# A four-layer image kernel, layer 0: the depthwise convolution of half the keys moves from TensorE to nine taps on VectorE

## The chip, the cores and the metric

The kernel runs on one core of one Trainium2 chip. Its time is the device time of one execution in microseconds (us); lower is better. A "span" is the time from the first to the last instruction in one profiled execution.

## What is computed

The reference takes two images of 128 channels by 64 x 64 pixels and adds four layers to them, one after the other. Only layer 0 is touched here. Cut to what matters:

```python
xn  = biasfree_ln(group_norm(x), ln1_w)              # per pixel, over the 128 channels
qkv = einsum('oi,bihw->bohw', w_qkv, xn)             # 1x1: 128 -> 5*128 channels
qkv = conv(qkv, w_dw, 3x3, 'SAME', groups=5*128)     # depthwise: each channel by its own 9 taps
q1, k1, v, q2, k2 = split(qkv, 5)                    # groups 0..4 of 128 channels
q1, q2, k1, k2 = l2norm over the 4096 pixels, per channel
out = softmax(q1 k1^T * temperature) v + v softmax(q2^T k2 * temperature)
x   = x + conv1x1(biasfree_ln(conv1x1(out, w_po)), w_proj) + b_proj
```

All is float32. A depthwise convolution of one group and one half of an image (32 of the 64 rows) is called a piece here: 128 channels, 2048 output pixels, nine taps each.

## The kernel before

`_layer0` handles the two images in turn. For each it calls `convolutions` (the 1x1 and depthwise parts, called the convolution stage below), then `attention`, and last `finish` (output projections and the residual). `finish` of image 0 is not run at once: it is a generator, passed as `before` into the convolution stage of image 1 and stepped there.

**Pieces on TensorE.** Eight pieces, in the list `order`: `(1,0), (1,1), (0,0), (0,1), (3,0), (4,0), (3,1), (4,1)`, as (group, half); group 0 is q1, 1 is k1, 3 and 4 are q2 and k2. For each piece `pointwise` computes the 1x1 product into PSUM on TensorE (L1553) and ScalarE copies it into a frame in SBUF with a rim of zeros (L1560; POOL clears the rim, L1543 to L1546). A frame's product is called P below. Then `depthwise` computes the piece with 144 matmuls of 32 x 32 diagonal blocks (L1575), called D below, into two PSUM tiles: `ps[0]` and `ps[1]`. A diagonal block on another row strip of TensorE puts its rows at another place, so the results of q1 and k1 are put in order by `in_place`: eight ScalarE copies out of `ps[0]`, eight VectorE copies out of `ps[1]` (L1595), with four of each before and four after the next frame's first half. q2 and k2 stay permuted and are copied whole by `copy` (L1586), which alternates between ScalarE and VectorE. `squares` (L1600, ScalarE) sums the squares for the norms.

**Pieces on VectorE.** The two pieces of v (group 2) are computed by `value_taps` on VectorE, straight from two frames of the tag `vpad` into `v`: one multiplication (L1611) and eight multiply-and-adds in place (L1613), each over 128 x 2048 elements. `convolutions` steps this generator a fixed number of times at the end of each turn n of its loop, `(0, 0, 3, 3, 4, 4, 4, 0)[n]`.

**PSUM.** The pool `spp` has three buffers of two banks each, tag `sp`. Each P takes two of them in turn (and one column block of `acc0`), each D two at once; so a D can only start when two of the three are free, and a P needs one after the other.

**Order.** The context `_in_order` chains the instructions of each of TensorE, VectorE, ScalarE and POOL in the order in which the program issues them. What stands in one engine's queue behind a waiting instruction therefore waits as well. The order of `convolutions` is thus the order on each engine: in turn n the depthwise piece n, the frame of piece n+2, copies, squares; in turn 0 also both frames of v and six steps of `before`; in turn 1 the rest of `before`; in turn 3 the norms (`inverse_norm`, `sc`); in turn 4 the scaling of q1; in turns 5 to 7 the channel products (`products`) and the transposes of v (`value_tiles`); at the end of the turn the taps.

Of the kernel before, what the change touches and what calls it, by code (L numbers as in the profile page):

```python
# [12 lines left out]
ALU = mybir.AluOpType  # L13
# [3 lines left out]
B, C, H, W = 2, 128, 64, 64  # L17
S = H * W
CH = 512
# [1416 lines left out]
def _layer0(ctx, tc, X, a, cst, worst, there, dram):  # L1436
    nc = tc.nc
# [6 lines left out]
    def sp():  # L1444
        return spp.tile([128, 2, CH], F32, tag="sp", name="ps_sp")

    def acc(n):
        return accp.tile([128, CH], F32, tag=f"acc{n}", name=f"ps_acc{n}")
# [25 lines left out]
    k1 = one.tile([128, S], F32, name="k1")  # L1474
    v = one.tile([128, S], F32, name="v")
# [62 lines left out]
    def frame(pool, tag="pad", bufs=2):  # L1538
        return pool.tile([128, H // 2 + 2, W + 2], F32, tag=tag, name=tag, bufs=bufs)

    def pointwise(pad, grp, half):

        nc.gpsimd.memset(pad[:, :, 0:1], 0.0)  # L1543
        nc.gpsimd.memset(pad[:, :, W + 1 : W + 2], 0.0)
        edge = 0 if half == 0 else H // 2 + 1
        nc.gpsimd.memset(pad[:, edge, :], 0.0)  # L1546
        first, to = (0, 1) if half == 0 else (H // 2 - 1, 0)
        for r0 in range(0, H // 2 + 1, 2 * ROWS):
            n = min(2 * ROWS, H // 2 + 1 - r0)
            ps = sp() if n > 1 else acc(0).rearrange("p (o c) -> p o c", o=1)  # L1550
            for i in range(0, n, ROWS):
                rows = min(ROWS, n - i)
                nc.tensor.matmul(  # L1553
                    ps[:, i // ROWS, : rows * W],
                    w_qkv[:, grp * C : (grp + 1) * C],
                    xn[:, (first + r0 + i) * W : (first + r0 + i + rows) * W],
                    start=True,
                    stop=True,
                )
            nc.scalar.copy(  # L1560
                pad[:, to + r0 : to + r0 + n, 1 : W + 1],
                ps.rearrange("p k (h w) -> p (k h) w", w=W)[:, :n, :],
            )
            yield
# [32 lines left out]
    def squares(pool, t, at):  # L1597
        junk = pool.tile([128, 2 * CH], F32, tag="junk", name="junk", bufs=1)
        n = t.free_size()
        nc.scalar.activation(junk[:, :n], t, AF.Square, accum_out=at)  # L1600

    def value_taps(pads):

        for half in range(2):
            cols = slice(half * S // 2, (half + 1) * S // 2)
            out = v[:, cols].rearrange("p (h w) -> p h w", w=W)
            for t in range(9):
                x = pads[half][:, t // 3 : t // 3 + H // 2, t % 3 : t % 3 + W]
                tap = wd[:, 18 + t : 19 + t]
                if t == 0:  # L1610
                    nc.vector.tensor_scalar_mul(out, x, tap)  # L1611
                else:
                    nc.vector.scalar_tensor_tensor(out, x, tap, out, ALU.mult, ALU.add)  # L1613
                yield

    def value_tiles(half):
        for i in range(2):
            ps = sp()
            t0 = 16 * half + 8 * i
            for t in range(8):  # L1620
                nc.tensor.transpose(
                    ps[:, t // 4, t % 4 * 128 : (t % 4 + 1) * 128],
                    v[:, (t0 + t) * 128 : (t0 + t + 1) * 128],
                    ident,
                )
            copy(vt[:, t0 : t0 + 8, :], ps.rearrange("p k (t c) -> p (k t) c", c=C))
            yield

    def products(pool, qk, half, gram):

        tok = {}
        for r in range(5):
            if r < 4:
                ps = sp()
                for n in range(2):
                    for t in range(4):
                        nc.tensor.transpose(
                            ps[:, n, t * 128 : (t + 1) * 128],
                            qk[:, n, r, t * 128 : (t + 1) * 128],
                            ident,  # L1640
                        )
                tok[r] = pool.tile([128, 2, CH], F32, tag="tok", name="tok", bufs=2)
                copy(tok[r], ps)
            if r >= 1:
                x = tok.pop(r - 1)
                for t in range(4):
                    nc.tensor.matmul(
                        gram[:, (r - 1) * 128 : r * 128],
                        x[:, 1, t * 128 : (t + 1) * 128],
                        x[:, 0, t * 128 : (t + 1) * 128],  # L1650
                        start=(half == 0 and r == 1 and t == 0),
                        stop=(half == 1 and r == 4 and t == 3),
                    )
            yield

    def convolutions(pool, b, before):


        ss = small.tile([128, 2, 4], F32, tag="ss", name="ss")
        ss2 = small.tile([128, 2, 4, 2], F32, tag="ss2", name="ss2")  # L1660
        gram = acc(1)
        order = [(1, 0), (1, 1), (0, 0), (0, 1), (3, 0), (4, 0), (3, 1), (4, 1)]
        frames = [frame(pool) for _ in range(2)]
        for n in range(2):
            run(pointwise(frames[n], *order[n]))
        pads = [frame(pool, "vpad") for _ in range(2)]
        taps = value_taps(pads)
        qk = None
        for n, (grp, half) in enumerate(order):
            ps = depthwise(grp, frames.pop(0))  # L1670
            following = iter(())
            if n + 2 < len(order):
                frames.append(frame(pool))
                following = pointwise(frames[-1], *order[n + 2])
            if grp >= 3:
                if grp == 3:
                    qk = pool.tile([128, 2, 4, CH], F32, tag="qk2", name="qk2", bufs=1)
                for p in range(2):
                    copy(qk[:, grp - 3, 2 * p : 2 * p + 2, :], ps[p])
                run(following)  # L1680
                for r in range(4):
                    squares(pool, qk[:, grp - 3, r, :], ss2[:, grp - 3, r, half : half + 1])
            else:
                out = (q1, k1)[grp]
                in_place(ps, half, out, 0)
                next(following, None)
                in_place(ps, half, out, 1)
                run(following)
                for i in range(2):
                    at = 2 * half + i  # L1690
                    squares(
                        pool, out[:, at * 2 * CH : (at + 1) * 2 * CH], ss[:, grp, at : at + 1]
                    )
            if n == 0:
                for half in range(2):
                    run(pointwise(pads[half], 2, half))
                for _ in range(6):
                    next(before, None)
            elif n == 1:
                run(before)  # L1700
            if n == 5:
                run(products(pool, qk, 0, gram))
            elif n == 6:
                run(value_tiles(0))
            elif n == 7:
                run(value_tiles(1))
                run(products(pool, qk, 1, gram))
            if n == 3:
                nq = inverse_norm(ss[:, 0, :], "nq1")
                nk = inverse_norm(ss[:, 1, :], "nk1")  # L1710
                sc = small.tile([128, 1], F32, tag="sc", name="sc")
                nc.vector.scalar_tensor_tensor(sc, nq, nk, temp, ALU.mult, ALU.mult)
            if n == 4:
                for c in range(0, NCH, 2):
                    cols = slice(c * CH, (c + 2) * CH)
                    nc.vector.tensor_scalar_mul(q1[:, cols], q1[:, cols], sc)
            for _ in range((0, 0, 3, 3, 4, 4, 4, 0)[n]):
                next(taps, None)

        own = small.tile([128, 4, C], F32, tag="own", name="own", bufs=1)  # L1720
        nc.vector.tensor_mul(
            own,
            gram.rearrange("p (r c) -> p r c", r=4),
            blocks.unsqueeze(1).to_broadcast([128, 4, C]),
        )
        return ss2, own
# [152 lines left out]
    def run(gen):  # L1879
        for _ in gen:  # L1880
            pass

    def chain(*gens):
        for g in gens:
            yield from g
# [3 lines left out]
    with _in_order(tc):  # L1889
        first = normalize(0)  # L1890
# [11 lines left out]
        wd = one.tile([128, 45], F32, name="wd")  # L1902
# [559 lines left out]
```

## Time and profile before

| | us |
|---|---|
| three runs | 4122.99, 4132.37, 4132.41 |
| median of the three | 4132.37 |
| the profiled execution's own time | 4122.99 |
| its span | 4121.1 |
| convolution stage of image 0, first L1553 to first L1370 (the attention's first matmul) | 39.45 to 190.08 |
| convolution stage of image 1, with the `finish` of image 0 in it | 798.64 to 997.57 |

The profile is one execution seen by the hardware profiler. Its timeline lists, per engine, runs of like instructions: start, length in us, engine, line, operation, output and inputs with their shapes, how many, and in brackets how long the engine stood idle just before them and whose result ended that wait. One float32 matmul of the program is recorded as two matmul records, so a D of 144 matmuls shows as x288. "PEclk" is the TensorE clock granted, as a share of full speed.

### The profile page before, as it was taken

What the parts mean: (1) busy time and instruction counts of PE and PEld (TensorE: products, weight loads), DVE (VectorE), ACT (ScalarE), POOL (GpSimd) and SP (SyncE); (2) the same over time, 40 slices, a digit from 0 to 9 for tenths busy, and PEclk for the clock granted to TensorE, in tenths of its full rate; (3) what the DMA queues carried; (4) which work ended last, traced back from release to release, by engine and by line L of the source; (5) the groups of instructions that cost most, each with busy time, mean ns of one, the idle gap of its engine ahead of it and who ended that gap; (6) DMA issues with size and microseconds to landing.
All of it is one profiled execution on the core that took longest, in us unless ns stands there. A gap on an engine that the chain in (4) does not pass through costs nothing. (4 is left out here: it accounts for less than half of the span.)

```text
span 4121.1 us, 83188 instructions
## 1 busy us (share of the span) xinstructions
PE 3944.4 (96%) x35790; PEld 1382.1 (34%) x35790; DVE 3183.8 (77%) x3526; ACT 3228.6 (78%) x3907; POOL 72.2 (2%) x145
## 2 busy tenths in 40 slices
PE   7999999989999998997898999999999999999998
PEld 4522222245222223445665332223222332222222
DVE  4689999747989998986775878767777777766666
ACT  4478888734888884334654899999999999999998
POOL 1001000000000001000000000000000000000000
PEclk9999999999999999998998999999999999999999
DMA  1199970000000000003673211111112011110000
GB/s 49 24 192 180 181 104 2 2 2 2 2 2 2 1 2 13 0 1 132 254 281 104 74 32 34 43 43 32 32 34 67 19 32 32 36 53 6 6 6 4
DMA packets 193133, 217.66 MB, mean 53 GB/s; under 512 B 30441, under 2 KB 154345, under 8 KB 188658
## 3 DMA queue, kind: packets, MB, share of 16 engines
q1 hardware_dynamic: 192754, 212.25, 20.2%
q8 instruction: 282, 4.62, 0.5%
q14 instruction: 97, 0.79, 0.1%
HBM read 178.64 MB, written 98.57 MB: 67 GB/s over the span
## 5 line engine op out<-in xcount | busy, mean ns | idle before, releaser
L2181 ACT ACTIVATE weights<-ps_s 128x1024 f32<-128x1024 f32 x1920 | 1780.6, 1078 | 93.8 <-PE ps_s L2167 93.7
L1379 ACT ACTIVATE weights<-ps_s 128x1024 f32<-128x1024 f32 x1024 | 992.9, 1023 | 169.3 <-PE ps_s L1370 151.1
L2190 PE MATMUL ps_acc<-weights,vt 128*32 128x512 f32 x8192 | 1094.5, 606 | 0.0
L1827 DVE TENSOR_TENSOR sums<-sums,weights 128x2048 f32<-128x2048 f32 x384 | 880.0, 2292 | 43.7 <-ACT weights L1379 7.4
L2167 PE MATMUL ps_s<-q,k 64*128 64x512 f32 x4096 | 838.4, 472 | 6.3 <-DVE exp_i L2123 3.0
L2167 PEld LDWEIGHTS ps_s<-q,k 64*128 64x128 f32 x4096 | 352.7, 184 | 948.4 <-ACT weights L2181 824.7
L1370 PE MATMUL ps_s<-q,k 32*64 32x512 f32 x8192 | 631.5, 614 | 3.7 <-ACT weights L1379 1.5
L1787 PE MATMUL ps_acc<-weights,vt 128*32 128x512 f32 x4096 | 550.0, 605 | 7.2 <-ACT used L1817 3.7
L2139 DVE SCALAR_TENSOR_TENSOR exp_z<-exp_z,exp_m 128x1024 f32<-128x1024 f32 x384 | 469.7, 1223 | 11.2
L2123 DVE TENSOR_SCALAR exp_i<-ps_s 128x1024 int32<-128x1024 f32 x128 | 156.7, 1224 | 254.0 <-PE ps_s L2167 253.1
L1370 PEld LDWEIGHTS ps_s<-q,k 32*64 32x64 f32 x8192 | 162.0, 130 | 435.1 <-PE ps_s L1370 337.9
L2190 PEld LDWEIGHTS ps_acc<-weights,vt 128*32 128x32 f32 x8192 | 161.9, 108 | 304.2 <-issue 303.4
L1787 PEld LDWEIGHTS ps_acc<-weights,vt 128*32 128x32 f32 x4096 | 81.1, 108 | 426.6 <-issue 403.1
L662 DVE SCALAR_TENSOR_TENSOR X<-g,w,X 128x2048 f32<-128x2048 f32 x84 | 197.4, 2351 | 2.6
L1827 DVE TENSOR_TENSOR sums<-weights 128x2048 f32<-128x2048 f32 x64 | 146.6, 2291 | 62.8 <-ACT weights L1379 62.6
L2143 DVE SCALAR_TENSOR_TENSOR weights<-exp_z,exp_i 128x1024 f32<-128x1024 f32 x128 | 156.7, 1224 | 13.9
L1575 PE MATMUL ps_sp<-pad,diag 32*32 32x512 f32 x4608 | 159.8, 600 | 2.3 <-ACT q L1595 1.3
L2139 DVE SCALAR_TENSOR_TENSOR exp_z<-exp_m 128x1024 f32<-128x1024 f32 x128 | 155.9, 1218 | 0.0
L1008 PE MATMUL ps_z<-w_ri,e 128*32 128x128 f32 x2048 | 137.4, 409 | 14.5 <-DVE e L950 12.4
L1575 PEld LDWEIGHTS ps_sp<-pad,diag 32*32 32x32 f32 x4608 | 95.3, 103 | 55.5 <-issue 17.1
L950 DVE TENSOR_SCALAR e<-ps_pe 32x136 f32<-32x136 f32 (+1 forms) x352 | 104.4, 297 | 5.0
L2213 DVE STREAM_TRANSPOSE z<-ps_acc 128x512 f32<-128x512 f32 x32 | 22.9, 717 | 104.1 <-PE ps_acc L2190 104.1
(296 smaller groups left out, 2886.8 us busy)
## 6 DMA issues: line engine op xcount, KB each, us to landing
w_ri<-w_r SPq DMA_DIRECT2D x16, 2112.0 KB, 8.1
w_ri<-w_i SPq DMA_DIRECT2D x16, 2112.0 KB, 13.6
stack<-qs SPq DMA_DIRECT2D x64, 256.0 KB, 2.0
q<-stack SPq DMA_DIRECT2D x128, 128.0 KB, 2.5
k<-stack SPq DMA_DIRECT2D x128, 128.0 KB, 2.6
stack<-ks SPq DMA_DIRECT2D x32, 256.0 KB, 2.2
w_r<-in_L_conv_kr_w SPq DMA_DIRECT2D x15, 528.0 KB, 13.1
w_r<-in_L_conv_kr_x SPq DMA_DIRECT2D x15, 528.0 KB, 12.9
```

The lines of the kernel that those rows point to most:

```text
L662: nc.vector.scalar_tensor_tensor(xi, g[:, i : i + H // 2, j : j + W], w8[:, s : s + 1], xi, ALU.mult, ALU.add)
L1370: nc.tensor.matmul(ps[j // 2][to, j % 2, :], k[rows, kt * 128 + 64 * half : kt * 128 + 64 * half + 64], q[rows, qb * CH : (qb + 1) * CH], ...
L1379: nc.scalar.activation(w[:, 2 * p : 2 * p + 2, :], ps[p], AF.Exp)
L1575: nc.tensor.matmul(ps[r // 2][to, r % 2, :].rearrange("p (h w) -> p h w", w=W), diag[rows, grp, t, :], pad[rows, y0 : y0 + ROWS, t % 3 : t ...
L1787: nc.tensor.matmul(ac[n][rows, :], lhs(rows), w[:, j, :], start=first, stop=last)
L1827: nc.vector.tensor_add(parts[0].rearrange("p j c -> p (j c)"), t.rearrange("p j c -> p (j c)"), w.rearrange("p j c -> p (j c)"),)
L2123: nc.vector.tensor_scalar(i, ps.rearrange("p j c -> p (j c)"), EXP_SCALE, EXP_BIAS, ALU.mult, ALU.add)
L2139: nc.vector.scalar_tensor_tensor(z, x, n, m, ALU.add, ALU.mult)
L2143: nc.vector.scalar_tensor_tensor(w.rearrange("p j c -> p (j c)"), z, EXP_TERMS[-1], power, ALU.add, ALU.mult)
L2167: nc.tensor.matmul(ps[j // 2][:, j % 2, :], g.k[kt // 4][rows, j // 2, keys], g.q[qb][rows, j // 2, :], start=True, stop=True,)
L2181: nc.scalar.activation(w[0], ps[p], AF.Exp)
L2190: nc.tensor.matmul(g.ac[32 * j : 32 * j + 32, :], g.vt[:, kt, j // 2, i : i + 2, :].rearrange("p a d -> p (a d)"), w[:, i, :], start=(at = ...
```

## The change

The first half of k1, piece (1,0), leaves `order`; seven pieces stay on TensorE. Its nine taps run on VectorE by `taps`, a more general form of `value_taps`, from a `vpad` frame straight into `k1`. Its frame is made first of all, and its first tap is issued ahead of turn 0. `vpad` has two buffers; the frame of the second half of v now takes over the buffer of the keys' frame, so it is made in turn 2 (`values_of(1)`) and no longer in turn 0. The squares of the first half of k1 are issued in turn 2, ahead of that frame. The tap schedule is now `(5, 5, 5, 4, 4, 4, 0)`, and all turn numbers after turn 0 are one lower than before.

```diff
-    def value_taps(pads):
-        for half in range(2):
-            cols = slice(half * S // 2, (half + 1) * S // 2)
-            out = v[:, cols].rearrange("p (h w) -> p h w", w=W)
...
+    def taps(grp, half, to, pad):
+        cols = slice(half * S // 2, (half + 1) * S // 2)
+        out = to[:, cols].rearrange("p (h w) -> p h w", w=W)
+        for t in range(9):
+            x = pad[:, t // 3 : t // 3 + H // 2, t % 3 : t % 3 + W]
+            tap = wd[:, 9 * grp + t : 9 * grp + t + 1]
+            if t == 0:
+                nc.vector.tensor_scalar_mul(out, x, tap)
+            else:
+                nc.vector.scalar_tensor_tensor(out, x, tap, out, ALU.mult, ALU.add)
+            yield
+
+    def squares_of(pool, out, half, at):
+        for i in range(2 * half, 2 * half + 2):
+            squares(pool, out[:, i * 2 * CH : (i + 1) * 2 * CH], at[:, i : i + 1])
...
-        order = [(1, 0), (1, 1), (0, 0), (0, 1), (3, 0), (4, 0), (3, 1), (4, 1)]
+        order = [(1, 1), (0, 0), (0, 1), (3, 0), (4, 0), (3, 1), (4, 1)]
+        kpad = frame(pool, "vpad")
+        run(pointwise(kpad, 1, 0))
+        first = taps(1, 0, k1, kpad)
         frames = [frame(pool) for _ in range(2)]
-        for n in range(2):
-            run(pointwise(frames[n], *order[n]))
-        pads = [frame(pool, "vpad") for _ in range(2)]
-        taps = value_taps(pads)
+        run(pointwise(frames[0], *order[0]))
+        next(first)
+        run(pointwise(frames[1], *order[1]))
+        by_vector = first
+
+        def values_of(half):
+            pad = frame(pool, "vpad")
+            run(pointwise(pad, 2, half))
+            return taps(2, half, v, pad)
...
             if n == 0:
-                for half in range(2):
-                    run(pointwise(pads[half], 2, half))
+                by_vector = chain(by_vector, values_of(0))
                 for _ in range(6):
                     next(before, None)
             elif n == 1:
                 run(before)
-            if n == 5:
+            if n == 4:
                 run(products(pool, qk, 0, gram))
...
-            if n == 3:
+            if n == 2:
+                squares_of(pool, k1, 0, ss[:, 1, :])
+                by_vector = chain(by_vector, values_of(1))
                 nq = inverse_norm(ss[:, 0, :], "nq1")
                 nk = inverse_norm(ss[:, 1, :], "nk1")
...
-            for _ in range((0, 0, 3, 3, 4, 4, 4, 0)[n]):
-                next(taps, None)
+            for _ in range((5, 5, 5, 4, 4, 4, 0)[n]):
+                next(by_vector, None)
```

More of the change, by code (lines that the diff above doesn't have):

```diff
@@ L1600, in squares @@
         nc.scalar.activation(junk[:, :n], t, AF.Square, accum_out=at)
-    def value_taps(pads):
-        for half in range(2):
-            cols = slice(half * S // 2, (half + 1) * S // 2)
-            out = v[:, cols].rearrange("p (h w) -> p h w", w=W)
[L1607 to L1614, printed above, removed]
+    def taps(grp, half, to, pad):
[12 more added lines that the diff above has]
+            squares(pool, out[:, i * 2 * CH : (i + 1) * 2 * CH], at[:, i : i + 1])
     def value_tiles(half):
@@ L1688, in convolutions @@
                 run(following)
[L1689 to L1693, printed above, removed]
+                squares_of(pool, out, half, ss[:, grp, :])
             if n == 0:
-                for half in range(2):
-                    run(pointwise(pads[half], 2, half))
+                by_vector = chain(by_vector, values_of(0))
                 for _ in range(6):
@@ L1700, in convolutions @@
                 run(before)
-            if n == 5:
+            if n == 4:
                 run(products(pool, qk, 0, gram))
+            elif n == 5:
+                run(value_tiles(0))
             elif n == 6:
-                run(value_tiles(0))
-            elif n == 7:
                 run(value_tiles(1))
                 run(products(pool, qk, 1, gram))
-            if n == 3:
+            if n == 2:
+                squares_of(pool, k1, 0, ss[:, 1, :])
+                by_vector = chain(by_vector, values_of(1))
                 nq = inverse_norm(ss[:, 0, :], "nq1")
@@ L1712, in convolutions @@
                 nc.vector.scalar_tensor_tensor(sc, nq, nk, temp, ALU.mult, ALU.mult)
-            if n == 4:
+            if n == 3:
                 for c in range(0, NCH, 2):
```

## The prediction

> **What bounds the kernel now.** First the busy line of the page, for the engine with the largest share:
>
> ```profile
> PE 3944.4 (96%) x35790; PEld 1382.1 (34%) x35790; DVE 3183.8 (77%) x3526; ACT 3228.6 (78%) x3907; POOL 72.2 (2%) x145
> ```
>
> TensorE is busy nearly throughout, VectorE for three quarters. But the shares average four layers, so next the timeline of the convolution stage of image 0, TensorE alone (D is x288, P is L1553):
>
> ```profile
> 71.50 9.77 PE L1575 MATMUL ps_sp<-pad,diag 32*32 32x512 f32 x288
> 81.20 1.98 PE L1553 MATMUL ps_sp<-xn,w_qkv 128*128 128x512 f32 x4
> 84.71 1.98 PE L1553 MATMUL ps_sp<-xn,w_qkv 128*128 128x512 f32 x4 [1.52 <-ACT pad L1560]
> 86.53 0.33 PE L1553 MATMUL ps_acc<-xn,w_qkv 128*128 128x64 f32 x2
> 87.18 9.77 PE L1575 MATMUL ps_sp<-pad,diag 32*32 32x512 f32 x288 [0.32 <-ACT k L1595]
> ```
>
> One turn of a q1 or k1 piece is 87.18 - 71.50 = 15.68 us: D 9.7, P with a wait for a PSUM buffer, 0.3 of waiting. TensorE hardly rests, so the stage is TensorE's. VectorE in the same stretch:
>
> ```profile
> 81.34 5.60 DVE L1595 COPY k<-ps_sp 32x512 f32<-32x512 f32 x8 [17.44 <-PE ps_sp L1575]
> 97.01 5.61 DVE L1595 COPY q<-ps_sp 32x512 f32<-32x512 f32 x8 [10.07 <-PE ps_sp L1575]
> 102.65 1.29 DVE L1611 TENSOR_SCALAR v<-vpad,wd 128x2048 f32<-128x2048 f32 x1
> 103.97 4.74 DVE L1613 SCALAR_TENSOR_TENSOR v<-vpad,wd,v 128x2048 f32<-128x2048 f32 x2
> ...
> 123.45 7.12 DVE L1613 SCALAR_TENSOR_TENSOR v<-vpad,wd,v 128x2048 f32<-128x2048 f32 x3
> ```
>
> VectorE copies for 5.6 us after each D and has some 10 us free in a turn: that is the cover for new taps. Three taps take 7.12, so 2.37 us each; the first, a plain multiplication, 1.29. Then ScalarE, for the squares that the change moves:
>
> ```profile
> 119.40 1.07 ACT L1600 ACTIVATE junk<-q 128x1024 f32<-128x1024 f32 x1
> 120.37 0.20 ACT L1600 ACTIVATION_READ_ACCUMULATOR junk<-q 128x1 f32 x1
> 120.60 1.06 ACT L1600 ACTIVATE junk<-q 128x1024 f32<-128x1024 f32 x1
> ```
>
> Two such squares come 1.20 us apart. Last the stage of image 1, where `finish` of image 0 lies between turns 0 and 1:
>
> ```profile
> 850.13 10.48 PE L1575 MATMUL ps_sp<-pad,diag 32*32 32x512 f32 x288
> 866.42 6.56 PE L1553 MATMUL ps_sp<-xn,w_qkv 128*128 128x512 f32 x8 [5.81 <-DVE k L1595]
> ```
> ```profile
> 853.06 0.15 DVE L1400 TENSOR_SCALAR ln_r<-ln_mv 128x4 f32<-128x4 f32 x1
> 860.67 5.60 DVE L1595 COPY k<-ps_sp 32x512 f32<-32x512 f32 x8 [7.46 <-PE ps_sp L1575]
> 866.31 0.69 DVE L1499 TENSOR_TENSOR y<-ps_sp,ln_r 128x512 f32<-128x512 f32 x1
> ```
>
> Here P can't start before VectorE's eight copies end: `finish` holds the third PSUM buffer and ScalarE's second half of `in_place` stands behind this P. And VectorE has only 7.46 us free before these copies.
>
> [...] 1.29 us for the first tap, 2.35 for the other (2341 to 2354 ns over all 32). [...] So taps delay the copies issued after them; 866.31, an operation that follows the copies at once, fits. [...] the eight 1x1 records after the 5.81 us wait take 6.56 us instead of 3.70, with a granted clock of 0.50 from 866 to 870 us.
>
> **The change, part by part** (image 0; D0 is the first remaining D).
> 1. One turn goes: -15.68. Its frame is now made ahead of D0, where P needs no wait (in 63 to 71 us two frames take 3.65 each): +3.65. Its 16 copies and 9.7 us of D go with the turn; the loss of VectorE's 5.6 is counted in the queue below.
> 2. The frame of v's second half leaves turn 0 (before: D0 at 48.47, D1 at 71.50, so 23.03). Now D1 needs P, two squares (2.25 on ScalarE) and the first copy of the one v frame left. That copy ends 19.8 after D0, 0.5 later than TensorE is ready: 19.85. So -3.18.
> 3. It arrives in turn 2, behind four squares on ScalarE, not two. Before, squares began 16.54 after that D's start (119.40 - 102.86). Four take 4.8; the copy of the new frame's first tile then ends at 16.54 + 4.8 + 0.9 = 22.25. The next D finds only one PSUM buffer free until then and starts at 22.3 instead of 15.65: +6.65, of which 3.7 is TensorE's work and 2.7 a new wait.
> 4. VectorE's queue. New: 1.29 + 8 x 2.37 = 20.2; gone: 5.6. Turn 0: the first tap runs under the next frame; copies (5.6) and five taps (11.85) are 17.45 in 19.85. Turn 1: 5.6 + 4 x 2.37 + 1.29 = 16.4 in 15.68; the copies of turn 2 come 0.6 late, but the frame that needs their buffer starts 17.4 after its D, and they end at 16.0. Turn 2: five taps begin when `sc` is done, at about 22.6, since the norm of k1 waits for the moved squares; they end 34.5 after D2 and the `qk` copy at 35.7. The next D would start at 22.3 + 13.49 = 35.8. Hidden, with 0.1 to spare. Later turns have 12.3 in 13.49, then less than before. So 0.
> 5. POOL clears one frame later and waits there for the last tap of k1; nothing waits for it, since ScalarE reaches that frame 10 us later. The set of DMAs is unchanged; the load of layer 2's weights, placed behind this stage, starts some 9 us earlier, and its busy slices end at about 620 us, far ahead of its use. 0.
>
> Sum: -15.68 + 3.65 - 3.18 + 6.65 = **-8.6 us** for image 0. Attention then begins that much earlier and runs unchanged.
>
> Image 1 has the same four terms, and one more. The five taps of turn 0 are issued after six steps of `finish`, so after 853.2, and end at 865.05. D1 ends at 860.6. VectorE's copies, P behind them (TensorE waits 10 us there, not 5.8), and all of `finish` behind P move by 865.05 - 860.67 = +4.4. Turn 1's taps follow `finish`; they make the copies of turn 2 2.2 late, which costs 0.3 on a P that has 2.7 to spare: 0. So about **-4.2 to -4.5**, I take -4.5.
>
> Together **-13.1 us**. The profiled execution's 4122.99 (span 4121.1 and 1.9 around it) becomes 4109.9. It is the fastest of the three runs; the median lies 9.4 above it. Against the median I forecast 4132.4 - 13.1 = **4119**.
>
> **Bounds of what the trace does not show.** Four squares ahead of a frame: the wait of 2.7 is at least 0 (if the buffer freed first is another one) and at most 2.7 + 1.0 (if it is the second tile's): 2.7 taken, since at that point two of the three buffers hold the new frame. Taps into k1: same shape as v's; -0.0 to +0.1 each. The clock: the same `products` work took 11.19 us in image 0 (145.40 to 156.59) and 14.06 in image 1 (950.01 to 964.07, clock 0.76), so a cold window costs 2.9. A shift of the stage can bring one or remove one, and the new wait in turn 2 may earn one: -2.9 to +8.7 over both images, 0 taken.
>
> **Rivals.** (a) All is hidden: the new waits do not come, in turn 2 and behind the taps in image 1. Then -13.1 - 2 x 2.7 - 4.4 = -23, to 4109. For it: VectorE is idle half of the stage. Against: the two waits follow from the order of the queues. Chance 0.10. (b) The clock takes part of it: two or three more cold windows, -13.1 + 6 to 8.7 = -4 to -7, to 4126. For it: image 1's 10 us wait and the new wait. Against: the 5.8 us wait was cold already. Chance 0.26. (c) Slower: VectorE becomes the bound. Turn 2 has 0.1 us to spare, turn 1 none, and in image 1 five taps stand bare; about 20 taps of both images would pay each rise of their pitch in full. At 3.0 us instead of 2.37 the gain is gone (20 x 0.65 = 13); at 3.7 it is 20 x 1.33 - 13.1 = +13.5, to 4146. For it: nothing beside ScalarE's squares over the same SBUF; against: v's taps, beside the same work, never took over 2354 ns. Chance 0.05. That the change does not do what it says is excluded: the order on each engine follows from the code.
>
> **How the numbers follow.** 0.3% of the median, about what a measurement of this kernel can tell from no change, is 12.4 us. My case (0.59) is centred 0.7 us beyond it: with the clock's windows I put 0.49 of it beyond and 0.10 within. Faster 0.49 + 0.10 (a) = 0.59; same 0.10 + 0.26 (b) = 0.36; slower 0.05. The low end, 4105, is my case from the fastest run (4110) with one cold window removed and 2 us for the terms' own errors; the high end, 4128, is (b) at the median with its smallest gain.
>
> **What would show it.** Right: the attention of image 0 begins at 181.5 instead of 190.1; 4032 records of L1575's matmuls (14 pieces of 288) instead of 4608; a D behind turn 2's frame released by ScalarE's `vpad` copy after about 2.7 us; the P of image 1 waiting about 10 us for VectorE's q copies. Wrong: no such wait (case a), PEclk under 0.8 in turns 2 and 3 (b), taps above 2.4 us or D released by VectorE (c).

## The result and the profile after

| us | before | changed | ratio, 95% interval |
|---|---|---|---|
| first measurement, medians of 6 and 6 runs | 4129.90 | 4111.35 | 0.9959 [0.9947, 0.9972] |
| second measurement, medians of 28 and 19 runs | 4124.17 | 4114.88 | 0.9978 [0.9970, 0.9986] |
| profiled execution, own time | 4122.99 | 4110.44 | |
| its span | 4121.1 | 4108.6 | |

The changed kernel is faster, by 0.4% in the first measurement and 0.2% in the second. The forecast was 4119.0 against 4132.4, a ratio of 0.9968; it lies between the two measurements, inside the first interval and just under the lower end of the second. The measured medians lie 7.7 and 4.1 us below the 4119.0. For the profiled pair the forecast was -13.1 us; the own times differ by -12.55, the spans by -12.5.

The page's busy line, of the changed kernel:

```profile
PE 3927.8 (96%) x35214; PEld 1371.9 (33%) x35214; DVE 3211.7 (78%) x3528; ACT 3220.2 (78%) x3891; POOL 74.8 (2%) x145
```

TensorE has 35790 - 35214 = 576 records fewer, two pieces of 288: one D in each image is gone. Its busy time fell by 16.6 us, VectorE's rose by 27.9. Next TensorE's timeline in the convolution stage of image 0 (start, length, engine, line, operation, count, and in brackets the wait and what ended it):

```profile
52.05 9.75 PE L1575 MATMUL ps_sp<-pad,diag 32*32 32x512 f32 x288
...
71.42 10.21 PE L1575 MATMUL ps_sp<-pad,diag 32*32 32x512 f32 x288
...
87.54 9.74 PE L1575 MATMUL ps_sp<-pad,diag 32*32 32x512 f32 x288 [0.32 <-ACT q L1595]
...
103.10 3.70 PE L1553 MATMUL ps_sp<-xn,w_qkv 128*128 128x512 f32 x8 [0.23 <-ACT q L1595]
106.64 0.33 PE L1553 MATMUL ps_acc<-xn,w_qkv 128*128 128x64 f32 x2
106.90 1.05 PE L1575 MATMUL ps_sp<-pad,diag 32*32 32x512 f32 x4
109.75 11.25 PE L1575 MATMUL ps_sp<-pad,diag 32*32 32x512 f32 x284 [1.80 <-ACT vpad L1560]
...
124.73 9.76 PE L1575 MATMUL ps_sp<-pad,diag 32*32 32x512 f32 x288
...
184.44 1.07 PE L1370 MATMUL ps_s<-q,k 32*64 32x512 f32 x2
```

D0, D1, D2, D3 and D4 start at 52.05, 71.42, 87.54, 106.90 and 124.73. The frame of v at 103.10 is the one that came into turn 2. The D behind it starts four records, then stands 1.80 us until ScalarE's `vpad` copy releases a PSUM buffer. The rest of that D takes 11.25 us instead of 9.7. The attention begins at 184.44 (before: 190.08; forecast: 181.5). ScalarE and VectorE around that wait:

```profile
107.64 1.06 ACT L1600 ACTIVATE junk<-k 128x1024 f32<-128x1024 f32 x1
108.61 0.19 ACT L1600 ACTIVATION_READ_ACCUMULATOR junk<-k 128x1 f32 x1
108.70 1.91 ACT L1560 COPY vpad<-ps_sp 128x1024 f32<-128x1024 f32 x2
```
```profile
87.33 7.13 DVE L1612 SCALAR_TENSOR_TENSOR k<-vpad,wd,k 128x2048 f32<-128x2048 f32 x3
...
98.05 5.61 DVE L1595 COPY q<-ps_sp 32x512 f32<-32x512 f32 x8
...
109.98 11.89 DVE L1612 SCALAR_TENSOR_TENSOR v<-vpad,wd,v 128x2048 f32<-128x2048 f32 x5
121.91 1.22 DVE L1586 COPY qk<-ps_sp 128x1024 f32<-128x1024 f32 x1
```

The frame's copies start at 108.70, the moment the fourth square is done. VectorE's five taps start at 109.98 and the `qk` copy behind them ends at 123.13, before D4 wants its buffer at 124.73. The taps of k run at the pitch of v's: 7.13 / 3 and 11.89 / 5, both 2.38 us.

Image 1, TensorE first, then VectorE, then ScalarE:

```profile
842.61 10.49 PE L1575 MATMUL ps_sp<-pad,diag 32*32 32x512 f32 x288
863.26 6.05 PE L1553 MATMUL ps_sp<-xn,w_qkv 128*128 128x512 f32 x8 [10.16 <-DVE q L1595]
...
886.85 9.76 PE L1575 MATMUL ps_sp<-pad,diag 32*32 32x512 f32 x288
...
906.65 1.05 PE L1575 MATMUL ps_sp<-pad,diag 32*32 32x512 f32 x4
910.25 9.73 PE L1575 MATMUL ps_sp<-pad,diag 32*32 32x512 f32 x284 [2.56 <-ACT vpad L1560]
```
```profile
845.54 0.15 DVE L1400 TENSOR_SCALAR ln_r<-ln_mv 128x4 f32<-128x4 f32 x1
845.60 11.89 DVE L1612 SCALAR_TENSOR_TENSOR k<-vpad,wd,k 128x2048 f32<-128x2048 f32 x5
857.51 5.60 DVE L1595 COPY q<-ps_sp 32x512 f32<-32x512 f32 x8
```
```profile
904.60 1.06 ACT L1600 ACTIVATE junk<-q 128x1024 f32<-128x1024 f32 x1 [1.07 <-DVE q L1595]
```

The five taps are squeezed in ahead of the copies, the copies come late, and P waits 10.16 us (5.81 before). In turn 2 the square of q waits 1.07 us for VectorE's late copy, so the wait at `vpad` is 2.56 and not 1.80.

Where the time went, from the starts in the timelines (a stage runs from its first P to the attention's first matmul, L1370):

| us | before | changed | difference |
|---|---|---|---|
| stage of image 0 | 150.63 | 144.39 | -6.24 |
| stage of image 1 | 198.93 | 192.38 | -6.55 |
| all else in the span | 3771.5 | 3771.8 | +0.3 |

So the gain is made in the two stages. The forecast for them was -8.6 and -4.5. That all else agrees to 0.3 us in this pair is chance: over the nine profiles of this document (the kernel before, the changed kernel twice, six experiments), whose code is the same there, it takes from 3771.5 to 3779.3 us.

### The profile page after: what moved, and what is told of

Read it like the earlier page. It is cut to its first block, busy times and chain, and to the rows that moved or that the text cites. A ratio compares the mean times of both kernels' runs of the same rounds, so it can differ in the third digit from the quotient of the medians.

```text
span 4108.6 us, 82016 instructions
## 1 busy us (share of the span) xinstructions
PE 3927.8 (96%) x35214; PEld 1371.9 (33%) x35214; DVE 3211.7 (78%) x3528; ACT 3220.2 (78%) x3891; POOL 74.8 (2%) x145
## 5 line engine op out<-in xcount | busy, mean ns | idle before, releaser
L1370 PE MATMUL ps_s<-q,k 32*64 32x512 f32 x8192 | 629.3, 612 | 4.6 <-ACT weights L1379 2.4
L2148 DVE SCALAR_TENSOR_TENSOR exp_z<-exp_z,exp_m 128x1024 f32<-128x1024 f32 x384 | 469.7, 1223 | 11.2
L1370 PEld LDWEIGHTS ps_s<-q,k 32*64 32x64 f32 x8192 | 161.6, 129 | 434.0 <-PE ps_s L1370 337.9
L1008 PE MATMUL ps_z<-w_ri,e 128*32 128x128 f32 x2048 | 137.5, 409 | 14.5 <-DVE e L950 12.1
L1575 PE MATMUL ps_sp<-pad,diag 32*32 32x512 f32 x4032 | 143.4, 603 | 5.4 <-ACT vpad L1560 4.4
L1575 PEld LDWEIGHTS ps_sp<-pad,diag 32*32 32x32 f32 x4032 | 84.8, 103 | 53.4 <-issue 13.5
```

The source lines that it names most:

```text
L1370: nc.tensor.matmul(ps[j // 2][to, j % 2, :], k[rows, kt * 128 + 64 * half : kt * 128 + 64 * half + 64], q[rows, qb * CH : (qb + 1) * CH], ...
L1575: nc.tensor.matmul(ps[r // 2][to, r % 2, :].rearrange("p (h w) -> p h w", w=W), diag[rows, grp, t, :], pad[rows, y0 : y0 + ROWS, t % 3 : t ...
L2148: nc.vector.scalar_tensor_tensor(z, x, n, m, ALU.add, ALU.mult)
```

## The experiments

Their measured times in one table; "stages" are the lengths of the two convolution stages in each kernel's profile. The second measurement of the changed kernel and the runs `e1`, `e2` and `e7` share one set of runs of the kernel before (median 4124.17), `e4`, `e5` and `e6` another (4123.22).

| kernel | median, us (runs) | ratio to before | stage 0 | stage 1 |
|---|---|---|---|---|
| changed, again | 4114.88 (19) | 0.9978 [0.9970, 0.9986] | 144.28 | 191.34 |
| e1, squares early | 4109.90 (7) | 0.9958 [0.9942, 0.9974] | 141.34 | 188.25 |
| e2, four taps first | 4108.55 (9) | 0.9961 [0.9948, 0.9973] | 144.58 | 189.38 |
| e4, own frame | 4120.51 (20) | 0.9993 [0.9986, 0.9999] | 148.12 | 197.93 |
| e5, no taps of k | 4108.88 (6) | 0.9964 [0.9951, 0.9978] | 143.96 | 188.66 |
| e6, more in turn 2 | 4125.69 (12) | 1.0006 [0.9997, 1.0014] | 149.18 | 199.37 |
| e7, norms last | 4104.22 (6) | 0.9953 [0.9936, 0.9970] | 138.98 | 185.48 |

Runs of one kernel scatter by 7 to 19 us, so for steps of 2 to 5 us the timelines decide, and the medians only accompany them. The stage lengths also contain changes of the clock that no edit aimed at: the first `products` of a stage, the same work in every kernel, took 11.2 us in 6 of the 18 profiled stages, 12.85 in 11 and 14.06 in one; in the profiles of the kernel before and of the changed kernel these lengths stand at granted clocks of 1.00, 0.87 and 0.76. Differences below are against "changed, again" unless said otherwise.

**The changed kernel again**, unaltered, as the yardstick.

> The changed kernel unaltered, as the reference point for the other runs of this group. Theory: 4108 to 4118 us, the convolution stage of image 0 (first L1553 to first L1370) 144 us and that of image 1 192 us[...].

Its stages (144.28, 191.34) repeat those of the first profile to 0.1 and 1.0 us. Its span, 4114.6, is nevertheless 6.0 us longer than the first profile's, and that lies outside the stages (3779.0 us against 3771.8). The median of 19 runs stands 9.3 us under the kernel before, not 18.5 as in the first measurement: the size of the gain on medians is known only to several us.

**e1: are the squares of k what makes turn 2 wait?**

```diff
             if n == 2:
-                squares_of(pool, k1, 0, ss[:, 1, :])
                 by_vector = chain(by_vector, values_of(1))
...
             for _ in range((5, 5, 5, 4, 4, 4, 0)[n]):
                 next(by_vector, None)
+            if n == 1:
+                squares_of(pool, k1, 0, ss[:, 1, :])
```

> The two squares of the first half of k1 move from turn 2, ahead of the frame of v, to the end of turn 1, where ScalarE is idle in image 0. Theory (the D after turn 2's frame waits for ScalarE, which stands behind four squares): that D starts 19.8 us after the D before it instead of 22.3, the wait on the vpad copy goes; -2.4 us in image 0. In image 1 the last k1 tap ends just as ScalarE should copy q, so the squares hold those copies by about 1: -1.4. Together about -4 us. Rival (VectorE's taps of turn 2 set the end in any case): sc comes no earlier, the next D waits for VectorE's qk copy instead, 0 us. Rival (the wait was PSUM alone, whatever ScalarE does): the D still starts 22 us later, 0 us.

The wait at ScalarE's `vpad` copy is gone, and a small one on VectorE shows. TensorE of this kernel, first in image 0, then at the first `products` of image 1:

```profile
106.66 10.23 PE L1575 MATMUL ps_sp<-pad,diag 32*32 32x512 f32 x288
...
121.20 9.78 PE L1575 MATMUL ps_sp<-pad,diag 32*32 32x512 f32 x288 [0.51 <-DVE qk L1586]
...
932.40 1.92 PE L1640 MATMUL ps_sp<-consts,qk 128*128 128x128 f32 x16
...
943.60 9.76 PE L1575 MATMUL ps_sp<-pad,diag 32*32 32x512 f32 x288
```

The stages shrink by 2.9 and 3.1. So the squares, not the frame, cost turn 2 its wait; with it gone, the D that stood at 11.25 us takes 10.23, and VectorE's queue is next in line, 0.51 us later than TensorE. Image 0 gained half a microsecond more than expected, since D3 also ran faster. Image 1 shrank by 3.1 and not by 1.4, but only half of that is the edit's: D2 to D4 took 35.41 us instead of 36.94, 1.5 less, as expected. The other 1.6 us came from `products`, which took 11.20 us (932.40 to 943.60) against 12.84; such lengths stood at granted clocks of 1.00 in the kernel before and 0.87 in the changed kernel.

**e2: the bare taps ahead of the copies in image 1.** One tap each of turns 0 and 1 is put off, to turns 4 and 5 (the last step of turn 5 had no tap left before).

```diff
-            for _ in range((5, 5, 5, 4, 4, 4, 0)[n]):
+            for _ in range((4, 4, 5, 4, 5, 4, 0)[n]):
                 next(by_vector, None)
```

> Schedule of taps (4, 4, 5, 4, 5, 4, 0) instead of (5, 5, 5, 4, 4, 4, 0): one tap less ahead of the copies that TensorE waits for in image 1. Theory (these taps stand bare there): TensorE's wait ahead of P falls from 10.2 us to 7.8, and the copies of turn 2 come earlier as well; image 1 -2.4 to -3.2, image 0 0. Rival (VectorE's queue is full all along, so a tap moved to a later turn costs there what it saves here): 0 us.

```profile
860.44 5.58 PE L1553 MATMUL ps_sp<-xn,w_qkv 128*128 128x512 f32 x8 [7.79 <-DVE q L1595]
...
905.32 11.28 PE L1575 MATMUL ps_sp<-pad,diag 32*32 32x512 f32 x284 [1.80 <-ACT vpad L1560]
```

P's wait falls from 10.16 to 7.79, by 2.37 (by 2.40 from the second profile's 10.19), the pitch of one tap: there each tap is paid in full. The wait at `vpad` in image 1 falls from 2.56 to 1.80, as in image 0, since VectorE's copies of turn 2 are no longer late. Of these 3.1 us the stage keeps 2.0; the D at 905.32 now ran at 11.28 instead of 9.73.

**e5: the same place, with the taps of k taken out.** This kernel leaves out taps 1 to 8 of the first half of k1, which then holds its first tap alone.

```diff
-        by_vector = first
+        by_vector = iter((None,) * 8)
```

> Taps 1 to 8 of k1 are left out, so the first half of k1 holds its first tap alone; eight empty steps keep the schedule of the other taps. Theory (the taps are hidden in image 0 and stand bare only in image 1, where five precede the copies that TensorE waits for): image 0 0 us, image 1 TensorE's wait 10.2 falls to 5.8 and the copies of turn 2 are on time: -4.4 to -5.5 in all. Rival (taps slow TensorE's or ScalarE's work beside them, or delay copies in every turn): -8 us or more, image 0 shorter too.

```profile
110.15 9.73 PE L1575 MATMUL ps_sp<-pad,diag 32*32 32x512 f32 x284 [1.79 <-ACT vpad L1560]
...
863.43 6.62 PE L1553 MATMUL ps_sp<-xn,w_qkv 128*128 128x512 f32 x8 [5.81 <-DVE q L1595]
```

P waits 5.81 us, exactly what it waited before the change. So the taps account for the whole 10.16 - 5.81 = 4.35 of added wait. The time from D1's start to D2's falls by less, 43.21 to 40.82, in good part because P behind the shorter wait runs slower (6.62 against 5.38); D2 was slower as well (10.63 against 9.76), so the stage gains 2.7 us and not the 4.4 to 5.5 expected. In image 0 the starts do not move: D0 to D1 takes 19.40 us (19.38 with the taps), D1 to D2 16.12 (16.11), and D3 resumes 22.22 after D2 (22.21). There all eight taps are hidden, which also speaks against the rival that eight more taps make VectorE the bound of image 0. The length of the whole stage says less, though it differs by only 0.3 us: D3, behind the same wait, took 9.73 us and not 11.24, and the front ahead of D0 12.93 and not 11.90.

**e6: how much room is in VectorE's turn 2?** Four multiply-and-adds of 128 x 1024, whose result nobody uses, behind the taps of turn 2.

```diff
                 next(by_vector, None)
+            if n == 2:
+                spare = pool.tile([128, 2, CH], F32, tag="tok", name="tok", bufs=2)
+                for _ in range(4):
+                    nc.vector.scalar_tensor_tensor(
+                        spare, k1[:, : 2 * CH], wd[:, 9:10], k1[:, : 2 * CH], ALU.mult, ALU.add
+                    )
```

> Four VectorE operations of 128 x 1024, whose result is not used, are added after the taps of turn 2 (about 5 us of VectorE per image). Theory (VectorE has 0.1 us to spare in turn 2): the D after next waits for VectorE's qk copy, +4.9 per image, +9 to +10 us in all. Rival (turn 2 is TensorE's and VectorE has room): 0 to +2 us.

TensorE's D3 and D4 and VectorE's added group, image 0:

```profile
109.43 11.23 PE L1575 MATMUL ps_sp<-pad,diag 32*32 32x512 f32 x284 [1.80 <-ACT vpad L1560]
...
128.12 12.36 PE L1575 MATMUL ps_sp<-pad,diag 32*32 32x512 f32 x288 [3.67 <-DVE qk L1586]
```
```profile
121.48 5.24 DVE L1731 SCALAR_TENSOR_TENSOR tok<-k,wd 128x1024 f32<-128x1024 f32 x4
126.75 1.23 DVE L1586 COPY qk<-ps_sp 128x1024 f32<-128x1024 f32 x1
```

5.24 us were added and D4 waits 3.67: 1.6 us of room in image 0, where D3 itself was slow (11.23). In image 1, where D3 takes 9.73, the wait is 5.17, so the room is 0.1 us, the margin that the prediction gave. The waits are followed by Ds of 12.36 and 11.54 us instead of 9.76. So the stages grew by 4.9 us, as expected, and by 8.0. The gain of the whole change is gone (1.0006 [0.9997, 1.0014]) with 2 x 5.24 = 10.5 us of added work on VectorE. So rival (c) was right that turn 2 has no room for slower taps; that the taps themselves would slow down was not seen.

**e4: was the frame of v in turn 2 a loss?** Here the keys' frame lies in the memory of `vt`, so that `vpad` serves v alone and both frames of v are made in turn 0, as before the change.

```diff
-        kpad = frame(pool, "vpad")
+        kpad = vt.rearrange("p n c -> p (n c)")[:, : (H // 2 + 2) * (W + 2)].rearrange(
+            "p (h w) -> p h w", w=W + 2
+        )
...
             if n == 0:
-                by_vector = chain(by_vector, values_of(0))
+                by_vector = chain(by_vector, values_of(0), values_of(1))
...
                 squares_of(pool, k1, 0, ss[:, 1, :])
-                by_vector = chain(by_vector, values_of(1))
                 nq = inverse_norm(ss[:, 0, :], "nq1")
```

> The frame of k1 is laid in the memory of vt, which is free until turn 5, so both frames of v have their own buffers and are made in turn 0 again; all else as in the changed kernel. Theory (VectorE's taps of turn 2, held by the norms, are as late as TensorE): turn 0 is 3.65 us longer; in turn 2 the next D starts 15.7 us after the one before instead of 22.3, but the D after it then waits some 6 us for VectorE's qk copy and begins where it did: +3.4 per image, about +7 us in all. Rival (the wait for the shared frame's PSUM buffer is the only thing in the way): +3.65 - 6.65 = -3 per image, -6 us.

```profile
105.81 10.13 PE L1575 MATMUL ps_sp<-pad,diag 32*32 32x512 f32 x288 [0.32 <-ACT q L1595]
115.87 3.70 PE L1553 MATMUL ps_sp<-xn,w_qkv 128*128 128x512 f32 x8
119.41 0.33 PE L1553 MATMUL ps_acc<-xn,w_qkv 128*128 128x64 f32 x2
125.89 11.60 PE L1575 MATMUL ps_sp<-pad,diag 32*32 32x512 f32 x288 [6.15 <-DVE qk L1586]
```
```profile
112.60 11.89 DVE L1612 SCALAR_TENSOR_TENSOR v<-vpad,wd,v 128x2048 f32<-128x2048 f32 x5
124.52 1.23 DVE L1586 COPY qk<-ps_sp 128x1024 f32<-128x1024 f32 x1
```

The wait on ScalarE is gone and one of 6.15 us on VectorE stands in its place: the five taps still start only when `sc` is done (112.60) and the `qk` copy behind them ends at 125.75, while TensorE, without the frame, is ready at 119.7. The stages grow by 3.8 and 6.6, where 3.4 each was expected; the slow D4s behind the new waits (11.60 and 11.47 instead of 9.76) are 1.8 and 1.7 of that. D2 to D4 takes 35.84 and 37.40 us without the frame, 37.18 and 36.94 with it, although the frame is 3.7 us of TensorE's work. In turn 2 the frame was not the cost; it was the work that covered VectorE's taps. This agrees with the first of the two cases written down and rules out the second.

**e7: a version from these.** The squares go behind the frame, the norms behind the taps, and the schedule is that of `e2`.

```diff
             if n == 2:
-                squares_of(pool, k1, 0, ss[:, 1, :])
                 by_vector = chain(by_vector, values_of(1))
-                nq = inverse_norm(ss[:, 0, :], "nq1")
-                nk = inverse_norm(ss[:, 1, :], "nk1")
-                sc = small.tile([128, 1], F32, tag="sc", name="sc")
-                nc.vector.scalar_tensor_tensor(sc, nq, nk, temp, ALU.mult, ALU.mult)
+                squares_of(pool, k1, 0, ss[:, 1, :])
...
-            for _ in range((5, 5, 5, 4, 4, 4, 0)[n]):
+            for _ in range((4, 4, 5, 4, 5, 4, 0)[n]):
                 next(by_vector, None)
+            if n == 2:
+                nq = inverse_norm(ss[:, 0, :], "nq1")
+                nk = inverse_norm(ss[:, 1, :], "nk1")
+                sc = small.tile([128, 1], F32, tag="sc", name="sc")
+                nc.vector.scalar_tensor_tensor(sc, nq, nk, temp, ALU.mult, ALU.mult)
```

> The schedule (4, 4, 5, 4, 5, 4, 0), the frame of v ahead of the squares of k1 in turn 2, and the norms (nq, nk, sc) after the taps of turn 2 instead of before them. Theory: both give-backs shrink: the D after the frame starts 19.8 us after the one before it in both images (-2.4 each), TensorE's wait in image 1 falls by 2.4, and VectorE's taps of turn 2 no longer wait for the norms: about -7 to -8 us against the changed kernel, so some 4101 to 4105. Rival (VectorE is the bound of these turns): at most -2.4.

TensorE and VectorE in image 0:

```profile
106.10 10.23 PE L1575 MATMUL ps_sp<-pad,diag 32*32 32x512 f32 x288
...
120.06 9.76 PE L1575 MATMUL ps_sp<-pad,diag 32*32 32x512 f32 x288
```
```profile
103.50 9.51 DVE L1612 SCALAR_TENSOR_TENSOR v<-vpad,wd,v 128x2048 f32<-128x2048 f32 x4
...
116.38 1.22 DVE L1586 COPY qk<-ps_sp 128x1024 f32<-128x1024 f32 x1 [1.70 <-PE ps_sp L1575]
```

Neither D waits. The taps no longer stand behind `sc`, end at 113, and VectorE now waits for TensorE (1.70), not the other way round. In image 1 P still waits 7.77 us behind four taps. The stages are 5.3 and 5.9 us shorter than in the changed kernel, and the median is 4104.22, 0.9953 [0.9936, 0.9970] of the kernel before. It is the lowest median here, and this version is faster than the kernel before and than the changed kernel measured beside it: its interval meets that one's only at its end, and the 11.2 us from the stages agree with the 10.7 between the medians. Expected were 7 to 8 us. Of the excess, 1.65 us is `products` of image 0 (11.20 instead of 12.85), and D3 of image 0 ran 10.23 instead of 11.24; so some of the gain is probably the clock's: in the first profile of the changed kernel a `products` of 12.85 stood at 0.87, and the slow D3 of 11.25 began at 0.58.

## Why the prediction was right

The total was right, and the mechanism was; the split over the images was off, through a term that was set to zero. Step by step:

1. **One turn gone, its P at the front.** Right: 576 records fewer. The front took 12.0 us from the first P to D0 in image 0 (8.98 to 9.02 before in the two images), so +3.0 and not +3.65, because the very first P of the stage took 4.59 us at a granted clock of 1.00 and not 5.26 as before, when the clock stood at 0.67; in image 1 12.64, so +3.66.
2. **v's second frame leaves turn 0.** Forecast D0 to D1 19.85. Measured 19.37, but D1 was 10.21 long, so D2 started 35.49 after D0 against a forecast of 19.85 + 15.68 = 35.53. Right; the 0.45 us by which D1 is longer than other Ds, at a granted clock of 1.00, is probably the wait for ScalarE's second `vpad` copy, inside D1 and not ahead of it: that copy ends at 72.76, and one weight load of D1 waits 0.3 us for ScalarE's `vpad` copy.
3. **The frame in turn 2.** Forecast: D held until 22.3 after D2, a wait of 2.7 on ScalarE's `vpad` copy. Measured: resumed at 109.75 - 87.54 = 22.2. The wait shows as 1.80 because four records ran first. `e1` shows that the squares were its cause.
4. **VectorE's queue.** "Hidden, with 0.1 to spare": `e6` shows 0.1 in image 1, and 1.6 in image 0, where D3 was slow. `e5` shows that without k's taps the distances from D0 to D1, to D2 and to D3's resuming change by no more than 0.02 us in image 0.
5. **The bare taps in image 1.** Forecast P's wait about 10, +4.4. Measured 10.16, +4.35; with the taps out, 5.81 (`e5`). The step behind it failed: late copies in turn 2 were said to fall on a P with 2.7 us to spare, "0". P did have it, but ScalarE's squares, queued behind the same copies, did not. They wait 1.07 us, the copies of v's frame begin 1.2 later after D2 than in image 0, and D3 resumes 910.25 - 886.85 = 23.4 after D2, not 22.3. `e2`, with one tap fewer, has no such wait. The step looked at TensorE's need for these copies and not at ScalarE's.

**The term that was mis-sized is the clock.** Stretches of lower clock (the prediction's cold windows, 2.9 us each by its estimate from `products`, 14.06 against 11.19) were bounded at -2.9 to +8.7 and taken as 0. Stretches of TensorE's work with their granted clock, first of the changed kernel, then of the kernel before (start:end, length, then busy time with its count for TensorE, its weight loads, VectorE, ScalarE and GpSimd; then granted clock, DMA share, GB/s):

```profile
109.75:113.00 3.25, 3.25 (x66) 1.39 (x68) 3.12 (x3) 0.97 (x2) 0.06 (x1) 0.58 0.00 0
113.00:117.00 4.00, 4.00 (x134) 2.96 (x130) 3.96 (x2) 0.00 (x0) 0.00 (x0) 0.91 0.02 4
138.00:150.90 12.90, 9.40 (x67) 8.92 (x65) 3.53 (x3) 5.82 (x12) 0.00 (x0) 0.87 0.00 0
937.20:950.00 12.80, 9.30 (x66) 8.77 (x64) 3.58 (x3) 5.82 (x12) 0.00 (x0) 0.87 0.01 1
```
```profile
145.40:156.60 11.20, 7.70 (x67) 7.15 (x67) 3.60 (x3) 5.83 (x12) 0.00 (x0) 1.00 0.00 0
891.00:901.50 10.50, 10.50 (x290) 5.87 (x289) 1.82 (x3) 0.00 (x0) 0.00 (x0) 0.92 0.01 3
950.00:964.00 14.00, 10.50 (x67) 10.03 (x65) 3.52 (x3) 5.83 (x12) 0.00 (x0) 0.76 0.00 0
```

Behind the new wait of image 0 the clock stands at 0.58, and D3 takes 1.5 us longer (11.25; 9.73 in image 1 at 1.00). The first `products` of image 0, 11.2 us at a clock of 1.00 before, take 12.85 at 0.87. Together about +3. In image 1 it went the other way: `products` fell from 14.06 at 0.76 to 12.85 at 0.87, D2 from 10.62 at 0.92 to 9.76 at 1.00, and P and what follows it in `finish` were about 1 us shorter: about -3.

With that, image 0's -8.6 becomes -6.24 after the -0.65 of step 1, and image 1's sum of terms, -4.16, becomes -6.55 after -0.5 on D0 to D1 and the 1.1 of step 5. The total was right to 0.6 us because two clock terms of 3 us cancelled, which was luck.

What lowers the clock was not shown. The length of the wait ahead of it does not settle it here: behind 1.80 us the clock was 0.58 in image 0 of the changed kernel, behind 2.56 us in its image 1 it was 1.00. The other profiles, by the length of the D behind such a wait: 11.24 us behind 1.80 and 9.73 behind 2.56 in the second profile, 9.73 and 9.72 behind 1.79 in the two images of `e5`. So it seems that the clock of a stage could not have been read from the profile of before; what decides it stays open.

**The level.** The forecast added the median's distance of 9.4 us to the profiled run. Medians of 28 and 32 further runs of the kernel before are 4124.17 and 4123.22, much nearer to the profiled run; the first three runs were two high and one low. Compared at like clock the difference is 14.5 (last section), near the forecast. The profiled pair's agreement to 0.6 us owes something to chance here too: the second profile of the changed kernel has -13.9 us in the stages, but +7.4 in all else, whose code did not change. Rival (a) is out: both waits came. Rival (b) came true in part in image 0, and its opposite in image 1. Rival (c) did not occur: the taps' pitch stayed at 2.38.

## What to carry to other kernels

When work moves from a full engine to one with idle time, its price lies, as it did here, where the new work stands in the queue ahead of something that another engine waits for: list for every late copy all its readers, not only the bound engine. A frame that looks like extra work may be the cover for other work; taking it out of turn 2 (`e4`) made the two stages 10.4 us longer. And put the new work ahead of a value that only a later step needs: in turn 2 TensorE waited for no tap once the taps no longer stood behind the norms (`e7`, which moved the squares as well).

## What the runs showed of the hardware

In turn 2 of the changed kernel the depthwise piece behind the frame did not wait for both of its PSUM tiles: it ran four matmul records (1.05 us; the two matmuls into `ps[0]`) and then stopped until ScalarE's copy had freed a buffer, so the bracketed wait (1.80) is shorter than the delay (2.85, from 106.90 to 109.75). The text ahead of the prediction had it starting only with both free.

The scatter of runs of an unchanged kernel goes with the mean TensorE clock that each run was granted. Over 28 runs of the kernel before, from 4113.4 to 4132.1 us, the clock went from 0.984 to 0.977; a line through them falls 2.25 us for each 0.001 of clock (correlation -0.91), and one through 19 runs of the changed kernel 3.15 us (-0.84). At 0.979 the two lines stand at 4127.5 and 4113.0, 14.5 apart, while the medians are 9.3 apart: the runs of the kernel before had the higher clock on the average, 0.9805 against 0.9785. Whether the change itself lowers the clock, by its new waits, or the runs merely fell so, was not tested. It stays open, and with it whether the gain at the median is nearer to 9 us or to 18.
